# Dividing softmax rows before they are turned, and writing out the order of VectorE and ScalarE, in the second attention of a two-layer network on one core

## The chip, the cores and the metric

One core of one Trainium2 chip, everything in fp32. The metric is the device time of the whole program in microseconds (us): lower is better. The program is one launch that computes a whole network of six parts, from an input of 4096 rows of 256 elements to an output of the same shape.

PE is the engine for matrix products and for transposes (a transpose is a product with the identity). DVE and ACT are the two vector engines: DVE does reductions and arithmetic on tiles, ACT does functions such as the exponential, which can add up its own outputs on the way, and copies. POOL does slower arithmetic and issues the indirect DMAs, SP issues ordinary DMAs. Each engine works through its own instructions in order and waits for the others by semaphores. PE writes into PSUM, of which a bank holds 128 x 512 elements here; the program has two pairs of banks for scores ("s"), three single banks that most other results take in turn ("m") and one for the attention's result ("z").

## The reference, cut to what is computed

```python
x = x + 0.5 * ffn0(ln(x)); x = x + attn0(ln(x)); x = x + 0.5 * ffn0(ln(x))
x = x + 0.5 * moe(ln(x)); x = x + attn1(ln(x)); x = x + 0.5 * moe(ln(x))

def attn1(x, w_q, w_k, w_v, w_o):          # x: 8 x 512 x 256, 16 heads of 64
    q = einsum("bsd,hdk->bhsk", x, w_q)    # k and v alike
    scores = einsum("bhqk,bhmk->bhqm", q, k) / 8
    z = einsum("bhqm,bhmk->bhqk", softmax(scores), v)
    return x + einsum("bse,ed->bsd", join_heads(z), w_o)

def moe(x, ...):                           # 16 experts in 4 groups, 4 chosen of each row
    weights, chosen = top4(softmax(x @ gate_w.T), within the two best groups)
    return sum(weights[e] * ((silu(x @ w1[e]) * (x @ w3[e])) @ w2[e])) + shared(x)
```

`ln` is the layernorm without scale and offset. There is no mask in `attn1`.

## The kernel before

**The six parts.** ffn0, the first attention, ffn0 again, then the first `moe` (the grouped FFN), the second attention and the second `moe`. The rows of the network, 32 tiles of 128 x 256, stay in the core's memory in `self.x`. The parts overlap at their ends. The first `moe` ends with 72 steps of collecting not yet done: for each tile of rows and each of four choices, POOL gathers the rows that an expert has left in DRAM (L1433), and two tiles later DVE adds them, times their weight, to `self.x` (L1452). These steps are handed to the second attention in the list `beside`. The second `moe` in its turn routes its first 20 of 32 tiles inside the second attention: class `Front` normalises rows on POOL (`normal`, `units`), `routing` is a generator of small steps, most of them on DVE, and `send` writes finished rows to the places of their experts by indirect DMAs.

**The second attention** (`_attn1`, L922 to L1162). It is worked in 64 chunks `n`; a chunk is one of eight sequences `b` and one of eight pairs of heads `c`. A chunk has two halves of two query tiles `qt` each. What a chunk needs:

- `heads(n)`: two projections, four matmuls of 128 x 512 each (q and k of two heads, L997), evicted to `qk`.
- `scores(g)` for half-chunk `g`: per query tile two products of 128 x 512 (L1023) into a pair of "s" banks; DVE takes the negated row maxima (L1029), ACT the exponentials of both heads with their row sums (L1032), into tiles `ex`. The exponentials are not divided by their sums.
- `turn(n, qt)`: for each of the two heads four transposes of 128 x 128 (L1044) into an "m" bank, which is evicted to `eT` by `evict`: DVE for head 0 (L189), ACT for head 1 (L187).
- `products(n)`: 16 matmuls (L1057) of the turned exponentials with v into the "z" bank, then the division. `run` takes the reciprocals of the chunk's sums on DVE and widens them on POOL (L1064) so that each stands 64 times; `scale` transposes these to a row per column (four transposes on PE, L1070), copies them out on ACT (L1074) and multiplies the result `zp` by them on DVE (L1076), into `zn`.
- once per sequence: `prepare(b)` normalises four tiles (L957), adds the normalised rows to `self.x` on POOL, turns them (two pieces) and projects v (eight pieces of two matmuls, L978). The moments of the layernorm are taken in lumps, with the first, fourth and sixth sequence (`ln_range`). `project(b)`, four pieces of eight matmuls (L1087), adds the output projection to `self.x`.

**What sets the order.** The loop at the end of `_attn1` is written under `tc.manual_schedule` for PE and POOL: these two run their instructions in the order in which the program writes them. For DVE and ACT a scheduler orders the instructions by its own estimates. In the loop, the scores stand one half ahead of the transposes that use them. In each half PE gets: the scores of the next half, (in a first half) the `products` of the chunk before, the first `turn`, (in a first half) `scale`, one piece of the list `fill`, the second `turn`, then more pieces of `fill`. `fill` holds the projections of the chunk after next, a part of `prepare` of the next sequence in six of eight chunks, the four pieces of `project` of the last sequence, and in five chunks the pieces of `Front.units`. The collecting steps are taken from `beside`, four in each first half from the second chunk on, with a hint that ties each addition to a maximum of the half before (`behind`). Routing takes six steps per chunk at once, after the 48th chunk (`ahead`), and `send` one tile of rows in each of the last 20 halves.

## Time and profile before

| | before |
|---|---|
| median of 3 runs | 4362.0 us |
| lowest, highest | 4359.38, 4363.59 us |
| the profiled execution | 4400.12 us |
| its span (first to last instruction) | 4398.4 us |
| its mean granted clock of PE | 0.915 |
| busy over the span | PE 87%, PE's weight loads 52%, DVE 44%, ACT 33%, POOL 28% |
| the second attention (L922 to L1162) in that span | about 2633 to 3930 us |
| the same stretch, 1297 us long | PE busy 1247.6, DVE 732.3, ACT 583.6, POOL 251.3 us |

The profiled execution is one run with the profiler on, and it lies 38 us above the median of the others. Its rows give, for each group of instructions, how often it ran, the busy time of all of them, the mean time of one in ns, and how long the engine stood idle just before them with what ended that ("the releaser"). A line number is the line of the kernel's source that wrote the instruction; helpers such as `evict` have one line for all their callers, so these groups are told apart by the names of tiles. A timeline's rows give start and length in us. A table of stretches gives the busy time of each engine between two moments of the span, PE's granted clock as a share of full speed, and how busy the DMA was.

### The profile page before, as it was taken

How to read it: one execution, taken by the hardware profiler on the slowest of the kernel's cores; microseconds unless marked ns; L12 is line 12 of the kernel's file. 1: busy time of each engine (PE TensorE's matmuls, PEld its weight loads, DVE VectorE, ACT ScalarE, POOL GpSimd, SP SyncE). 2: the span in 40 equal slices, each digit the busy share in tenths (PEclk: the TensorE clock that was granted, in tenths of full speed). 3: DMA queues.
4: the chain of work that ended last, by engine and by line, in shares of the span. 5: the costliest groups of instructions: out<-in, count | busy, mean ns of one | idle time of the engine just before them, and what ended most of it. 6: DMA issues, size and time to landing. Idle time of an engine off the chain costs nothing.

```text
span 4398.4 us, 51682 instructions
## 1 busy us (share of the span) xinstructions
PE 3847.5 (87%) x17660; PEld 2307.5 (52%) x17660; DVE 1956.4 (44%) x5201; ACT 1440.2 (33%) x3227; POOL 1227.8 (28%) x1132
## 2 busy tenths in 40 slices
PE   5799987999999669999678879999999999998877
PEld 5566563333334546566455754545545555556654
DVE  5221106555544431120564456665555556445354
ACT  2122222444433212222122324444444444443321
POOL 2323223333220123223154241220000111533164
PEclk9999997899985579999789999999999999999998
DMA  5223226500000313222434540110000000135453
GB/s 181 54 58 68 68 35 221 184 22 12 23 20 6 98 34 67 66 61 39 125 128 131 190 148 20 30 29 1 1 1 1 1 1 8 53 116 160 147 173 101
DMA packets 262993, 316.65 MB, mean 72 GB/s; under 512 B 31696, under 2 KB 232784, under 8 KB 262480
## 3 DMA queue, kind: packets, MB, share of 16 engines
q1 hardware_dynamic: 213584, 212.12, 15.5%
q0 software_dynamic: 49152, 101.24, 9.5%
q8 instruction: 146, 2.39, 0.2%
q14 instruction: 111, 0.91, 0.1%
HBM read 157.81 MB, written 147.06 MB: 69 GB/s over the span
## 4 chain that ended last, share of the span: by engine, by line
PE 57%; DVE 9%; issue 8%; ACT 5%; DMA 4%; POOL 2%; another core or an unknown queue 1%; POOLq 0%; DVEq 0%; ACTq 0%; SPq 0%
PE pq L997 5%; PE op L459 5%; PE sp L1023 5%; PE zp L1057 5%; PE hp L448 4%; PE tp L1044 4%; PE hs L1661 3%; PE st L769 3%; PE pv L978 3%; PE hp L1581 2%; PE yp L1087 2%; PE pp L637 2%; ACT ex L1032 2%; DMA acc_d<-ob,idx 2%; PE yps L1681 2%
## 5 line engine op out<-in xcount | busy, mean ns | idle before, releaser
L1032 ACT ACTIVATE ex<-sp,nmax 128x512 f32<-128x512 f32 x512 | 347.8, 689 | 410.9 <-DVE nmax L1029 386.0
L459 PE MATMUL op<-w,hid 128*128 128x256 f32 x2048 | 472.6, 394 | 0.0
L448 PE MATMUL hp<-exT,w 128*128 128x512 f32 x1024 | 448.7, 596 | 0.0
L459 PEld LDWEIGHTS op<-w,hid 128*128 128x128 f32 x2048 | 405.4, 199 | 66.8 <-issue 8.6
L1433 POOL DMA_INDIRECT yg<-ys_d,slot x256 | 264.6, 1034 | 523.4 <-DVE x L1452 246.5
L466 POOL DMA_INDIRECT acc_d<-ob,idx x128 | 199.8, 1561 | 689.0 <-ACT ob L465 391.3
L464 DVE TENSOR_TENSOR ob<-op,b 128x256 f32<-128x256 f32 x128 | 54.3, 424 | 664.0 <-PE op L459 490.2
L1661 PE MATMUL hs<-w_sb,xT 128*128 (+1 forms) x1152 | 321.5, 403 | 24.6 <-ACT xT L1648 9.3
L1029 DVE TENSOR_REDUCE nmax<-sp 128x2 f32<-128x1024 f32 x256 | 303.0, 1218 | 73.8 <-PE sp L1023 72.9
L1044 PEld LDWEIGHTS tp<-ident,ex 128*128 128x128 f32 x2048 | 226.8, 141 | 191.3 <-issue 129.4
L448 PEld LDWEIGHTS hp<-exT,w 128*128 128x128 f32 x1024 | 195.0, 192 | 233.0 <-issue 232.1
L1044 PE MATMUL tp<-ident,ex 128*128 128x128 f32 x2048 | 275.2, 277 | 37.0 <-ACT eT L187 36.5
L740 DVE CUSTOM_DVE_ANT_0 junk<-sp,mask 128x128 f32<-128x128 f32 (+3 forms) x512 | 248.5, 485 | 129.3 <-PE sp L733 109.5
L452 ACT ACTIVATE hid<-hp,b 128x512 f32<-128x512 f32 x256 | 176.0, 687 | 339.2 <-PE hp L448 338.2
L1023 PE MATMUL sp<-qk,qk 64*128 64x512 f32 x1024 | 261.4, 629 | 1.9 <-ACT ex L1032 1.9
L1250 POOL DMA_INDIRECT slots_d<-wide,slot x176 | 173.8, 988 | 298.5 <-DMA slots_d<-wide,slot 110.7
L997 PE MATMUL pq<-xnT,wide 128*128 128x512 f32 x512 | 252.0, 616 | 5.7 <-DVE eT L189 5.0
L778 ACT ACTIVATE ex<-st 128x1024 f32<-128x1024 f32 (+3 forms) x256 | 174.1, 704 | 243.0 <-DVE st L776 243.0
L1661 PEld LDWEIGHTS hs<-w_sb,xT 128*128 128x128 f32 x1152 | 206.0, 199 | 62.9 <-issue 22.4
L1057 PE MATMUL zp<-eT,v 128*64 128x512 f32 x1024 | 234.8, 600 | 0.3 <-DVE eT L189 0.3
L465 ACT ACTIVATE ob<-ob,gate 128x256 f32<-128x256 f32 x128 | 65.0, 508 | 510.0 <-DVE ob L464 482.6
L1064 POOL COPY wide<-rec 128x512 f32<-128x512 f32 x64 | 39.4, 616 | 669.6 <-PE rp L1070 572.3
(326 smaller groups left out, 6105.1 us busy)
## 6 DMA issues: line engine op xcount, KB each, us to landing
xs<-slots_d SPq DMA_DIRECT2D x70, 512.0 KB
ys_d<-ys SPq DMA_DIRECT2D x70, 512.0 KB
w<-in_W SPq DMA_DIRECT2D x32, 1024.0 KB
slots_d<-mask SPq DMA_DIRECT2D x8, 2304.0 KB
ys_d<-mask SPq DMA_DIRECT2D x8, 2304.0 KB
w_sb<-in_w SPq DMA_DIRECT2D x24, 512.0 KB
xn_d<-xn SPq DMA_DIRECT2D x16, 512.0 KB
acc_d<-x SPq DMA_DIRECT2D x8, 1024.0 KB
```

The source lines that it names most:

```text
L448: nc.tensor.matmul(hp, lhsT=w1[:, c, f * P : f * P + P], rhs=exT[e][:, c, h * CH : h * CH + CH], start=(c == 0), stop=(c == DC - 1),)
L459: nc.tensor.matmul(op, lhsT=hid[h][:, f, i * P : i * P + P], rhs=w2[:, f, :], start=(f == 0), stop=(f == FC - 1),)
L466: nc.gpsimd.indirect_dma_start(out=acc_d[:, :], out_offset=bass.IndirectOffsetOnAxis(ap=idx[:, e, st : st + 1], axis=0), in_=ob, in_offset ...
L740: nc.vector.tensor_tensor_reduce(out=junk[:, :wd], in0=sps[h // 2][:, h % 2, :wd], in1=mask[:, S - wd :], scale=1.0, scalar=NEG, op0=ALU.a ...
L997: nc.tensor.matmul(pp, lhsT=(wq, wk)[a][:, k, c * P : c * P + P], rhs=seq[b]["xnT"][:, k, :], start=(k == 0), stop=(k == DC - 1),)
L1023: nc.tensor.matmul(sp[:, j, :], lhsT=q[r, qt * P : qt * P + P], rhs=k[r, :], start=True, stop=True)
L1029: latest[0] = nc.vector.tensor_reduce(nmax, sp, AX.X, ALU.max, negate=True).ins
L1032: nc.scalar.activation(ex[:, j, :], sp[:, j, :], AF.Exp, bias=nmax[:, j : j + 1], accum_out=ch["sums"][:, qt, j : j + 1],)
L1044: nc.tensor.transpose(tp[:, k, :], ch["ex", qt][:, j, k * P : k * P + P], self.ident)
L1057: nc.tensor.matmul(zp[DK1 * j : DK1 * j + DK1, :], lhsT=seq[b]["v", h][:, k, at : at + DK1], rhs=ch["eT"][:, j, k, :], start=(k == 0), sto ...
L1433: inst = nc.gpsimd.indirect_dma_start(out=self.y[t][:, r, :], out_offset=None, in_=self.k.ys_d[:, :], in_offset=bass.IndirectOffsetOnAxis( ...
L1661: nc.tensor.matmul(hp.rearrange("p a i -> p (a i)"), lhsT=st[j]["xT"][:, c, :], rhs=self.w13[:, st[j]["e"], c, :].rearrange("p e i -> p (e ...
```

## The change

All of it is in the second attention and in how `Front` is fed; the mathematics is the same.

- **The division.** A new step `divide(i)` follows the exponentials of each query tile on DVE: a reciprocal of the two sums, and two multiplications of a 128 x 512 row in place, one per head. What the transposes read is then already the softmax. `scale`, the widened reciprocals, their transposes and the product after them are gone; `zp` goes to `zn` by a copy on ACT.
- **The order.** DVE and ACT are now in the manual schedule too, so the program's order holds for all four. To write that order, `scores` takes both maxima and then the exponentials of the first query tile; those of the second (`exps(1)`) stand after the first `turn`, `divide(0)` before the second `turn` and `divide(1)` at the end of the half.
- **The evictions** of turned tiles alternate by query tile and no longer by head: `evict(..., qt)`. The first `turn` of a half is evicted by DVE alone, the second by ACT alone.
- **The filling of PE.** A first half takes one piece of `fill` between its turns as before, and then half of what is over three; the second half takes the rest. `prepare` comes as a list for each chunk: the normalising, then both turned pieces, then one or two v pieces per chunk. `project` comes in two chunks, two pieces in each.
- **Normalising.** The moments of the layernorm are taken two tiles at a time at the ends of given chunks (`own`), and finished at the end of another.
- **Collecting.** The four steps stand in each second half, from the first chunk on, after the next scores and before the first `turn`; the hint is gone.
- **Routing.** One step at each of three places of a half, after `begin + groups`; `units` comes in chunks 43 to 47.

The diff, without empty lines, and cut (`...`) where `normal` only repeats the loop that stood in `norm`; the last change to `Front` removes `stats`, which `own` replaces.

```diff
@@ -943,24 +943,22 @@
         def prepare(b):
             st = seq[b] = {"z": []}
-            def norm(c):
+            def normal():
+                mv, rstd = stats
+                st["xn"] = work.tile([P, QT, D], F32, name="xn", bufs=1)
+                st["xnT"] = work.tile([P, DC, CH], F32, name="xnT")
+                for i in range(QT):
...
+                rows = self.x[:, b * QT : b * QT + QT, :]
+                nc.gpsimd.tensor_tensor(rows, rows, st["xn"], ALU.add)
+            def turned(c):
                 def run():
-                    mv, rstd = stats
-                    if c == 0:
-                        if b in (0, 3, 5):
-                            self.ln_range(pool, stats, b * QT, {0: 3, 3: 2, 5: 3}[b] * QT)
...
-                        rows = self.x[:, b * QT : b * QT + QT, :]
-                        nc.gpsimd.tensor_tensor(rows, rows, st["xn"], ALU.add)
                     tp = psum.tile([P, CH], F32, name="tpn", tag="m", bufs=3)
                     for i in range(QT):
                         nc.tensor.transpose(
@@ -982,9 +980,10 @@
                     nc.vector.tensor_copy(st["v", h][:, i, :], pp)
                 return run
-            return [norm(c) for c in range(DC)] + [
-                value(i, h) for h in range(HK // CH) for i in range(QT)
-            ]
+            v = [value(i, h) for h in range(HK // CH) for i in range(QT)]
+            return [[normal], [turned(0), turned(1)], v[0:2], v[2:3], v[3:4], v[4:6], v[6:7], v[7:8]]
         def heads(n):
             b, c = divmod(n, NC)
@@ -1009,11 +1008,10 @@
         def scores(g):
             n, half = divmod(g, 2)
             ch, q, k = chunk[n], chunk[n][0], chunk[n][1]
-            if half == 0:
-                ch["sums"] = work.tile([P, QT, 2], F32, name="sums", bufs=3)
-            sps = []
+            sps, nmax, sums = [], [], []
             for i in range(2):
                 qt = 2 * half + i
                 sp = psum.tile([P, 2, CH], F32, name="sp", tag="s", bufs=2)
@@ -1024,15 +1022,28 @@
                         sp[:, j, :], lhsT=q[r, qt * P : qt * P + P], rhs=k[r, :], start=True, stop=True
                     )
             for i, sp in enumerate(sps):
-                qt = 2 * half + i
-                nmax = work.tile([P, 2], F32, name="nmax", bufs=4)
-                latest[0] = nc.vector.tensor_reduce(nmax, sp, AX.X, ALU.max, negate=True).ins
-                ex = ch["ex", qt] = work.tile([P, 2, CH], F32, name="ex", bufs=4)
+                m = work.tile([P, 2], F32, name="nmax", bufs=4)
+                nc.vector.tensor_reduce(m, sp, AX.X, ALU.max, negate=True)
+                nmax.append(m)
+                sums.append(work.tile([P, 2], F32, name="sums", bufs=4))
+                ch["ex", 2 * half + i] = work.tile([P, 2, CH], F32, name="ex", bufs=4)
+            def exps(i):
                 for j in range(2):
                     nc.scalar.activation(
-                        ex[:, j, :], sp[:, j, :], AF.Exp,
-                        bias=nmax[:, j : j + 1], accum_out=ch["sums"][:, qt, j : j + 1],
+                        ch["ex", 2 * half + i][:, j, :], sps[i][:, j, :], AF.Exp,
+                        bias=nmax[i][:, j : j + 1], accum_out=sums[i][:, j : j + 1],
                     )
+            def divide(i):
+                rec = work.tile([P, 2], F32, name="rec", bufs=2)
+                nc.vector.reciprocal(rec, sums[i])
+                for j in range(2):
+                    row = ch["ex", 2 * half + i][:, j, :]
+                    nc.vector.tensor_scalar(row, row, rec[:, j : j + 1], None, ALU.mult)
+            exps(0)
+            return exps, divide
         def turn(n, qt):
             ch = chunk[n]
@@ -1042,12 +1053,13 @@
                 tp = psum.tile([P, QT, P], F32, name="tp", tag="m", bufs=3)
                 for k in range(QT):
                     nc.tensor.transpose(tp[:, k, :], ch["ex", qt][:, j, k * P : k * P + P], self.ident)
-                self.evict(ch["eT"][:, j, :, qt * P : qt * P + P], tp, j)
+                self.evict(ch["eT"][:, j, :, qt * P : qt * P + P], tp, qt)
         def products(n):
             b, c = divmod(n, NC)
             ch = chunk[n]
+            box = []
             def run():
                 zp = psum.tile([P, CH], F32, name="zp", tag="z", bufs=1)
@@ -1058,25 +1070,14 @@
                             zp[DK1 * j : DK1 * j + DK1, :], lhsT=seq[b]["v", h][:, k, at : at + DK1],
                             rhs=ch["eT"][:, j, k, :], start=(k == 0), stop=(k == QT - 1),
                         )
-                rec = work.tile([P, QT, 2], F32, name="rec", bufs=3)
-                nc.vector.reciprocal(rec, ch["sums"])
-                wide = work.tile([P, QT, 2, DK1], F32, name="wide", bufs=1)
-                nc.gpsimd.tensor_copy(wide, bc(rec, 3, DK1))
-                ch["wide"], ch["zp"] = wide, zp
-            def scale():
-                rp = psum.tile([P, CH], F32, name="rp", tag="m", bufs=3)
-                for qt in range(QT):
-                    nc.tensor.transpose(
-                        rp[:, qt * P : qt * P + P], ch["wide"][:, qt].rearrange("p h d -> p (h d)"), self.ident
-                    )
-                rs = work.tile([P, CH], F32, name="rs", bufs=1)
-                nc.scalar.copy(rs, rp)
+                box.append(zp)
+            def out():
                 zn = work.tile([P, CH], F32, name="zn", bufs=9)
-                nc.vector.tensor_tensor(zn, ch["zp"], rs, ALU.mult)
+                nc.scalar.copy(zn, box[0])
                 seq[b]["z"].append(zn)
-            return [run, scale]
+            return [run, out]
         def project(b):
             def out(i):
@@ -1094,70 +1095,95 @@
             return [out(i) for i in range(QT)]
         front = Front(self, after, ctx)
-        latest = [None]
         def row_psum(cols):
             t = psum.tile([P, CH], F32, name="row", tag="m", bufs=3)
             return t[:, :cols]
-        steps = after.routing(0, front.lg, front.pool, row_psum, lambda: None)
+        known = []
+        steps = after.routing(0, front.lg, front.pool, row_psum, lambda: known.append(True))
         groups = after.parts[0] // QT
-        def ahead(n):
-            i = n - (NC * groups + 2)
-            if i == 0:
-                front.stats()
-            elif 1 <= i <= groups:
-                return front.units(i - 1, row_psum)
-            elif groups < i:
-                advance(steps, 6)
-            return []
-        with tc.manual_schedule(engines={mybir.EngineType.PE, mybir.EngineType.Pool}):
-            for piece in prepare(0) + heads(0) + heads(1):
+        def moments(pool, stats, t):
+            return lambda: self.ln_moments(pool, stats, t, 2)
+        own = {}
+        for first, tiles, n in ((3 * QT, 2 * QT, 10), (5 * QT, 3 * QT, 25)):
+            for t in range(0, tiles, 2):
+                own[n] = moments(pool, stats, first + t)
+                n += 1
+            own[n] = lambda first=first, tiles=tiles: self.ln_finish(pool, stats, first, tiles)
+        begin = NC * groups + 2
+        for t in range(0, after.parts[0], 2):
+            own[33 + t // 2] = moments(front.pool, after.stats, t)
+        last = own[begin]
+        own[begin] = lambda: (last(), self.ln_finish(front.pool, after.stats, 0, after.parts[0]))
+        E = mybir.EngineType
+        with tc.manual_schedule(engines={E.PE, E.DVE, E.Activation, E.Pool}):
+            self.ln_range(pool, stats, 0, 3 * QT)
+            for piece in sum(prepare(0), []) + heads(0) + heads(1):
                 piece()
-            scores(0)
-            fill, tail, behind = [], [], None
+            exps, divide = scores(0)
+            exps(1)
+            divide(0)
+            divide(1)
+            fill, tail = [], []
             coming = prepare(1)
             for n in range(N):
                 b, c = divmod(n, NC)
                 if c == 0:
-                    coming = prepare(b + 1) if b + 1 < B else []
+                    coming = prepare(b + 1) if b + 1 < B else [[]] * NC
                 if n + 2 < N:
                     fill += heads(n + 2)
-                if c not in (3, 4):
-                    fill += coming[:2]
-                    coming = coming[2:]
-                fill += ahead(n)
+                fill += coming[c]
+                if 1 <= n - begin <= groups:
+                    fill += front.units(n - begin - 1, row_psum)
+                def ahead():
+                    if n > begin + groups:
+                        advance(steps, 1)
                 for half in range(2):
                     g = 2 * n + half
                     if g + 1 < 2 * N:
-                        scores(g + 1)
+                        exps, divide = scores(g + 1)
                     if half == 0 and tail:
                         tail.pop(0)()
-                    if half == 0 and n > 0:
+                    if half == 1:
                         for _ in range(min(TOPK, len(beside))):
-                            beside.pop(0)(behind)
-                    t = 2 * n + half - 2 * N + after.parts[0]
+                            beside.pop(0)()
+                    t = g - 2 * N + after.parts[0]
                     if t >= 0:
+                        assert known
                         front.send(t)
-                    behind = latest[0]
                     turn(n, 2 * half)
+                    more = g + 1 < 2 * N
+                    if more:
+                        exps(1)
                     if half == 0 and tail:
                         tail.pop(0)()
+                    ahead()
                     if fill:
                         fill.pop(0)()
+                    if more:
+                        divide(0)
                     turn(n, 2 * half + 1)
-                    left = 2 - half
-                    for _ in range(-(-len(fill) // left)):
+                    ahead()
+                    for _ in range(len(fill) if half else max(0, len(fill) - 3) // 2):
                         fill.pop(0)()
+                    if more:
+                        divide(1)
+                    ahead()
+                if n in own:
+                    own[n]()
                 tail = products(n)
-                if c == 0 and b > 0:
-                    fill += project(b - 1)
+                if b > 0 and c < 2:
+                    fill += project(b - 1)[2 * c : 2 * c + 2]
             for piece in tail + project(B - 1):
                 piece()
@@ -1815,9 +1841,6 @@
         self.lg = self.pool.tile([P, f.parts[0], E1], F32, name="chosen")
         self.xn = {}
-    def stats(self):
-        self.k.ln_range(self.pool, self.f.stats, 0, self.f.parts[0])
     def normal(self, t, n):
         if t % QT == 0:
```

## The prediction

> **What bounds the kernel now.** First the stages: busy time in stretches of the span. The second attention runs from 2633 to 3930 us; nothing else is edited, so I read only that.
>
> ```profile
> core 0: us, PE busy (x) PEld busy (x) DVE busy (x) ACT busy (x) POOL busy (x), PEclk, DMA share, GB/s
> 2660.00:2821.00 161.00, 154.83 (x724) 77.11 (x722) 107.65 (x173) 83.59 (x205) 41.10 (x43) 0.99 0.09 27
> 3135.00:3291.00 156.00, 152.14 (x714) 80.78 (x712) 82.44 (x114) 71.08 (x178) 7.24 (x9) 1.00 0.00 1
> 3600.00:3797.00 197.00, 186.62 (x868) 98.26 (x868) 124.55 (x203) 88.17 (x221) 47.75 (x50) 0.97 0.06 22
> ```
>
> PE is busy 97% at full clock in the middle line, DVE 53% (67% in the first, where the collecting of the FFN before is mixed in). PE sets this stage: a microsecond counts if it leaves PE's line. So next PE's timeline over one chunk (two heads of one sequence; 64 in all), and its waits from 2660 to 3945:
>
> ```profile
> 3821.61 3.65 PE L1057 MATMUL zp<-eT,v 128*64 128x512 f32 x16
> 3825.20 1.09 PE L1044 MATMUL tp<-ident,ex 128*128 128x128 f32 x8
> 3826.13 0.60 PE L1070 MATMUL rp<-ident,wide 128*128 128x128 f32 x4
> 3826.64 1.99 PE L997 MATMUL pq<-xnT,wide 128*128 128x512 f32 x4
> 3828.46 1.04 PE L1044 MATMUL tp<-ident,ex 128*128 128x128 f32 x8
> 3829.34 1.96 PE L997 MATMUL pq<-xnT,wide 128*128 128x512 f32 x4
> 3831.23 1.99 PE L1023 MATMUL sp<-qk,qk 64*128 64x512 f32 x8
> 3833.14 1.53 PE L1044 MATMUL tp<-ident,ex 128*128 128x128 f32 x12
> 3835.64 0.66 PE L1044 MATMUL tp<-ident,ex 128*128 128x128 f32 x4 [0.97 <-ACT eT L187]
> 3836.22 1.99 PE L1023 MATMUL sp<-qk,qk 64*128 64x512 f32 x8
> ```
>
> ```profile
> PE tp L1044 <- ACT eT L187: 36.5, 37, 2.0
> PE pq L997 <- DVE eT L189: 5.0, 4, 2.6
> ```
>
> From start to start: zp 3.59, eight transposes 0.9, rp 0.51, a projection 1.85, four score matmuls 1.92. There is one hole: the last four transposes find no free bank, because ACT's eviction stands behind exponentials. Sixteen transposes take 3.08 there (3833.14 to 3836.22) where two undisturbed eights take 1.80: 1.28 lost, 37 times. Last the groups of the same stretch that price DVE, and a timeline at 661:
>
> ```profile
> L1029 DVE TENSOR_REDUCE nmax<-sp 128x2 f32<-128x1024 f32 x254 | 300.7, 1218 | 73.4 <-PE sp L1023 72.5 <-issue 0.7
> L1452 DVE SCALAR_TENSOR_TENSOR x<-yg,coef,x 128x256 f32<-128x256 f32 x72 | 34.5, 479 | 1.1
> L957 DVE TENSOR_SCALAR xn<-x,mv,rstd 128x256 f32<-128x256 f32 x24 | 9.2, 406 | 0.0
> ```
>
> ```profile
> 661.45 3.48 DVE L159 TENSOR_SCALAR y<-mv 128x4 f32<-128x4 f32 x1
> 661.64 0.54 POOL L576 MEMSET widek<- 128x512 f32 x1
> ```
>
> **What the Trainium skill says.** VectorE: DVE Perf Modes, section "The perf-mode tier table": fp32 tensor_scalar in SBUF runs two elements per cycle; its errata section measures some 150 cycles fixed, so my estimate for 128x512 is (256+150)/0.96 = 0.42 us. The trace has no such shape; 128x256 with two pointer scalars takes 0.406, which at one element per cycle would leave 0.14 fixed, at two 0.27. I take 0.49, bounds 0.42 and 0.69 (the trace's 128x512 DVE reads from PSUM). SBUF — State Buffer, "Who interferes with whom": such an instruction and a GpSimd one exclude each other. The trace agrees: the 128x4 one above took 3.48 us (median of its line 0.17), until POOL's row of memsets ended at 664.9. TensorEngine Tiling (Array Packing), "Key Properties": a change of tiling mode drains TensorE. The trace shows weight loads 0.76 apart at such changes against 0.24; the change keeps all five of a chunk.
>
> **Removed.** Four rp transposes per chunk, on PE's line: 64 x 0.51 = 32.6. POOL's copy (0.62), ACT's rs copy (0.59, replaced by an equal zn copy) and DVE's zn product and reciprocal (0.69 + 0.20) are not on PE's line: no gain.
>
> **The stalls of 1.28.** Now one projection is placed in each half between the two eights, so sixteen never stand together; the evictions of the first eight are both DVE's, of the second both ACT's, and these stand after both exponentials. Does a new wait replace it? Walk through a half with times from PE's start of scores. DVE reads scores at 1.18 (timeline: 3831.23 to 3832.40), two maxima end at 3.55, evictions of the first eight at 4.2 and 4.85. PE does scores to 1.92, eight transposes to 2.85, projection to 4.7, then needs the bank freed at 4.2, the next at 5.15 (freed 4.85): slack 0.4 and 0.3, no stall. ACT: exponentials 2.4 to 5.2, then its evictions, needed a half later. The scaled rows are needed a half later too. So all of 37 x 1.28 = 47 goes. The few DVE waits (5.0) go as well: sum of gains 85.
>
> **Added on DVE.** A division of a tile: reciprocal 0.17 and two products, 0.49 long but about 0.42 apart: 1.1 us, four per chunk, less 0.9 removed: +3.5 on 82.4/8 = 10.3, so 13.8 against a chunk of about 18.4 (74%). In bulk it lies beside PE. It could delay the maxima: in the first half of a chunk (9.2 long on PE, since zp stands in it) DVE's two divisions end at 7.5 + 2.2 = 9.7, the next half needs it at 10.4. At 0.69 per product 10.9, 0.5 late, 0.1 stall after the slack: at most 6 us over all. Cost taken: 0.
>
> **Moved: the FFN's additions.** 72 of them, four in each second half of chunks 0 to 17, now written between the maxima and the evictions. Before, a scheduler put them in DVE's gaps. Queued behind them: the evictions, and behind those PE's next transposes. The four are chained, 0.5 each (the group's mean is 0.479): first eviction ends at 3.55 + 2.0 + 0.65 = 6.2 instead of 4.2, where PE wants it at 4.7: 1.5, and 0.2 more for the projection's bank. 18 x 1.7 = 31 lost. Bounds: 0.9 each (16) if PE is late there anyway, 2.2 (40) if the gathers' data come late. The gathers themselves, on POOL, only start half a chunk earlier: 0.
>
> **Moved: normalisation and routing.** Moments go to the ends of chunks, two tiles (1.15) each: behind them stand the next maxima, with zp's 3.6 on PE before anything is needed: 0. The three finishing pieces wait for ACT's root behind its evictions; same cover, 2 in all. Normal rows of a sequence start POOL's 2.36 us sum just before a division: 8 times, in a half with slack: 0; POOL's four rows per group of the next FFN (4.84 together) hold divisions up to 2.5: 5 times, I take 1 each, 5. Routing: three steps per half over six chunks, by their rows (0.5 to 1.5 each) some 30 us on DVE, 4.5 to 5 per chunk: DVE then has 18 to 19 against PE's 16.5, and the maxima of the second half begin 2 late. I count 3 in four chunks, 1 in the two whose output projection gives DVE time, 3 for the step with two 128x640 products (2 x 2.3): 17. The lump before cost about 4 beyond the 2.6 counted above; net 13, bounds 4 and 25. The start has one division more before PE's first transposes: 2. The sends of the last ten chunks: POOL needs 7.1 per half (1.22 + 5.76), PE's halves average 7.4; divisions wait up to 1.2 for its rows: 2, and the next FFN's load still has the output projection as cover. SP's queue is unchanged in order.
>
> **Sum.** Gains 85, losses 31 + 2 + 5 + 13 + 2 + 2 = 55: net 30. The profiled execution took 4400.12 (span 4398.4, 1.7 around it), so 4370 in its terms; it lies 38 us over the median of 4362.0, and the 30 us of a stage at full clock I carry over unscaled: 4332.
>
> **Rivals.** (1) The additions cost little, because PE reaches that place late or DVE has caught up: their 31 falls to about 5, routing to 5: 85 - 5 - 5 - 11 = 64, 4298. For it: slack in first halves; against: the order is fixed, maxima cannot begin before 1.18. (2) Order costs more than I see: 0.4 us of slack per half is thin, and if every chunk loses 0.45 to a bank, 64 x 0.45 = 29 brings it to 4361, the same. For it: DVE's maxima and evictions now decide each transposition; against: the walk. (3) Slower: the divisions are the bound. Mechanism: a product of 1.0 us (held by POOL or by waiting for its own reciprocal) makes a division 2.2, the first half's end at 11.9, the maxima 1.5 late, PE 1.1 short in the 48 chunks without output projection: 53 lost, 4385. It decides from about 0.8 per product on: there the loss has taken 30. Against it: L957's 0.406 and no POOL work in chunks 18 to 40. (4) PE was never the limit, and DMA or the gathers end the stage: 97% busy and 1 GB/s speak against it; no number of its own, within the same band.
>
> **Numbers.** Mine 0.55 (4312 to 4350), rival 1 0.20, rival 2 0.13, rival 3 0.10, rival 4 0.02. Range 4290 to 4366: rival 1 with its lower bounds at the bottom, rival 2 at the top. 0.2% (9 us) is about what a measurement can tell from no change: faster than 4353 has 0.55 + 0.20 and a part of rival 2, 0.78; the same 0.11; slower 0.11.
>
> **What would show it.** No rp rows; PE's wait for ACT's eviction near zero; plain chunks of about 14.8 us between zp starts (16.5 now), 147 to 148 per eight against 156; in the first two sequences instead PE waiting for DVE's evictions, about 1.7 per chunk, and eight chunks in 161 to 163; products at 0.42 to 0.5; PE waits on DVE where routing stands. Wrong if the middle sequences do not fall below 150, if products take 0.7 or more, or if a stall per chunk stands in front of the second eight everywhere.

## The result, and the profile after

The changed kernel takes 4328.22 us (median of 6 runs, 4315.64 to 4344.49) against 4359.69 before (6 runs): a ratio of 0.9934, interval [0.9912, 0.9957]. The profiled execution took 4328.61, its span 4326.9. The two profiled spans differ by 71.5 us, but only part of that is the change: 41 us of it lie after the last zp, in the last FFN, which is not edited and where PE was granted 0.91 of its clock before and 0.94 after. (That end takes 488 us before and 447 after, but among the changed kernel's variants below it also ranges from 445 in e1 to 486 in e8.) So from here on the measure is a stretch that holds the edited loop and runs nearly at full clock: from the start of the first zp to the start of the last, chunk by chunk. It is 1233.5 us before and 1205.7 after, 27.8 less; the forecast had 30.

The eight sequences of that stretch, in us (the first has no output projection of an earlier sequence in it; the last has seven steps from zp to zp, the others eight):

| sequence | 1 | 2 | 3 | 4 | 5 | 6 | 7 | 8 | sum |
|---|---|---|---|---|---|---|---|---|---|
| what else is in it | collecting | collecting | collecting's end | | | units | routing | sends | |
| before | 143.7 | 156.6 | 157.4 | 156.0 | 156.0 | 183.8 | 161.8 | 118.4 | 1233.5 |
| after | 148.5 | 163.8 | 149.2 | 147.9 | 147.9 | 176.7 | 159.1 | 112.7 | 1205.7 |

First the busy times in three stretches, the first with collecting, the second without other work, the third with routing:

```profile
core 0: us, PE busy (x) PEld busy (x) DVE busy (x) ACT busy (x) POOL busy (x), PEclk, DMA share, GB/s
2660.00:2821.00 161.00, 147.73 (x668) 70.58 (x668) 127.12 (x234) 78.89 (x198) 36.61 (x35) 0.99 0.09 27
3135.00:3283.00 148.00, 147.36 (x684) 76.92 (x680) 111.00 (x216) 72.41 (x180) 2.37 (x1) 1.00 0.00 1
3608.00:3767.00 159.00, 151.54 (x688) 77.33 (x686) 133.76 (x259) 69.31 (x177) 54.41 (x47) 1.00 0.09 31
```

In the middle line PE is still the bound, at 147.36 of 148 us, and DVE has gone from 53% to 75%. In the first line PE is busy 92% where it was 96% before: something new stops it there, while DVE works 127 of 161 us. PE's timeline over one plain chunk of the changed kernel, from zp to zp, shows the new order; it answers to the timeline of before:

```profile
3268.79 3.65 PE L1069 MATMUL zp<-eT,v 128*64 128x512 f32 x16
3272.38 1.09 PE L1055 MATMUL tp<-ident,ex 128*128 128x128 f32 x8
3273.31 1.88 PE L996 MATMUL pq<-xnT,wide 128*128 128x512 f32 x4
3275.03 1.04 PE L1055 MATMUL tp<-ident,ex 128*128 128x128 f32 x8
3275.99 1.99 PE L1021 MATMUL sp<-qk,qk 64*128 64x512 f32 x8
3277.91 1.09 PE L1055 MATMUL tp<-ident,ex 128*128 128x128 f32 x8
3278.84 1.88 PE L996 MATMUL pq<-xnT,wide 128*128 128x512 f32 x4
3280.56 1.04 PE L1055 MATMUL tp<-ident,ex 128*128 128x128 f32 x8
3281.53 1.99 PE L1021 MATMUL sp<-qk,qk 64*128 64x512 f32 x8
```

No row of rp, no row of 12 and 4 transposes, no idle time in brackets: 14.65 us to the next zp at 3283.44. PE's waits over the whole attention, the first three that concern the loop:

```profile
PE tp L1055 <- DVE eT L189: 32.5, 24, 2.7
...
PE pq L996 <- ACT qk L1002: 4.5, 10, 1.6
PE tp L1055 <- ACT qk L1002: 3.9, 3, 1.3
```

The wait for ACT's evictions (36.5 us, 37 times) is gone, and one for DVE's evictions stands in its place, 32.5 us, 24 times. From 2660 to 2986 alone, the two sequences with collecting, it is 21.2 us, 15 times; in the three sequences after them there is none, and the rest lies in the last three. The two groups of DVE that are new:

```profile
L1043 DVE TENSOR_SCALAR ex<-ex,rec 128x512 f32<-128x512 f32 x508 | 241.9, 518 | 9.0
L1040 DVE RECIPROCAL rec<-sums 128x2 f32<-128x2 f32 x254 | 39.4, 155 | 0.7 <-ACT ex L1033 0.7
```

A multiplication is 0.49 us long (the median; the mean is 0.518), and two of them in a row take 0.88: the second starts 0.40 after the first. With the reciprocal a division is 1.07 us, forecast 1.1. The Trainium skill's page VectorE: DVE Perf Modes, section "The perf-mode tier table", which gives such an operation two elements per cycle in SBUF, is borne out: at one element per cycle 512 elements alone would be 0.53 (512/0.96, an estimate with the clock of that page), more than the whole operation takes.

### The profile page after: what moved, and what is told of

The parts are those of the page before. It is cut to its first block, busy times and chain, and to the rows that moved or that the text cites. A ratio compares the mean times of both kernels' runs of the same rounds, so it can differ in the third digit from the quotient of the medians.

```text
span 4326.9 us, 51707 instructions
## 1 busy us (share of the span) xinstructions
PE 3805.9 (88%) x17404; PEld 2269.2 (52%) x17404; DVE 2148.3 (50%) x5841; ACT 1431.6 (33%) x3227; POOL 1197.4 (28%) x1068
## 4 chain that ended last, share of the span: by engine, by line
PE 30%; DVE 7%; issue 6%; DMA 5%; POOL 3%; ACT 2%; POOLq 0%; DVEq 0%; ACTq 0%; SPq 0%
PE zp L1069 5%; PE sp L1021 4%; PE tp L1055 4%; PE pq L996 4%; DMA yg<-ys_d,slot 3%; PE pv L976 3%; PE yp L1088 2%; POOL slots_d L1276 2%; PE hs L1687 2%; DVE nmax L1026 2%; PE hp L1607 1%; ACT ex L1033 1%; POOL yg L1459 1%; DVE x L1478 1%; PE yps L1707 1%
## 5 line engine op out<-in xcount | busy, mean ns | idle before, releaser
L1055 PE MATMUL tp<-ident,ex 128*128 128x128 f32 x2048 | 280.4, 279 | 37.0 <-DVE eT L189 32.5
L1043 DVE TENSOR_SCALAR ex<-ex,rec 128x512 f32<-128x512 f32 x512 | 243.7, 518 | 9.0
L996 PE MATMUL pq<-xnT,wide 128*128 128x512 f32 x512 | 241.9, 597 | 5.6 <-ACT qk L1002 4.5
```

Of the source, the lines that this page charges most:

```text
L996: nc.tensor.matmul(pp, lhsT=(wq, wk)[a][:, k, c * P : c * P + P], rhs=seq[b]["xnT"][:, k, :], start=(k == 0), stop=(k == DC - 1),)
L1055: nc.tensor.transpose(tp[:, k, :], ch["ex", qt][:, j, k * P : k * P + P], self.ident)
```

## The experiments

Three questions tell the prediction's account from its rivals. Is the removed PE work worth its own time, and nothing else lost for it? Did the order of the turns end the stall, or who evicts? And what costs the time in the first two sequences, the place of the additions or DVE's load? Three groups of runs were made, each with runs of the kernel before beside them; that kernel took 4359.2, 4411.0 and 4404.6 us there, so between groups only ratios and the stretch compare. A ratio is of medians; the sequences are those of one profiled execution of each kernel.

In that execution PE's granted clock drops to one half for 3.4 us or 6.8 us at a time, and its matmuls then take about twice as long (one of zp 1.11 us at most, 0.59 otherwise). Such a stretch costs PE at most half its length. The last column gives the sum of these halves, from the trace's records of the clock: an estimate, and an upper bound, of what each sequence owes to its clock. Sequences 4 and 5 have none in any kernel, and of the third sequences only that with doubled products has one (1.7). Whether a kernel's waits bring the drops about is not shown. All times in us:

| kernel | ratio to before, interval | sequences 1, 2 | 4, 5 | 6 | 7 | 8 | stretch | at most from the clock, sequences 1, 2, 6, 7, 8 |
|---|---|---|---|---|---|---|---|---|
| before | 1 | 143.7, 156.6 | 156.0, 156.0 | 183.8 | 161.8 | 118.4 | 1233.5 | 0, 0, 6.8, 1.7, 0 |
| changed | 0.9934 [0.9912, 0.9957] | 148.5, 163.8 | 147.9, 147.9 | 176.7 | 159.1 | 112.7 | 1205.7 | 0, 1.7, 5.1, 0, 0 |
| e1 additions later | 0.9871 [0.9854, 0.9887] | 135.7, 147.9 | 147.9, 147.9 | 173.4 | 159.1 | 115.3 | 1175.6 | 0, 0, 1.7, 0, 3.4 |
| e2 order alone | 1.001 [1.0, 1.002] | 155.8, 167.7 | 152.1, 152.1 | 172.9 | 158.4 | 111.7 | 1223.1 | 1.7, 1.7, 0, 0, 0 |
| e3 order left to scheduler | 0.9952 [0.9939, 0.9966] | 157.0, 149.0 | 149.0, 149.0 | 178.4 | 160.4 | 110.0 | 1201.9 | 6.8, 0, 10.2, 1.7, 0 |
| e4 evicted by head | 0.9951 [0.9933, 0.9969] | 143.7, 157.4 | 148.9, 148.9 | 185.6 | 162.3 | 114.2 | 1210.2 | 0, 0, 8.5, 1.7, 1.7 |
| e5 turns together | 1.0175 [1.0158, 1.0192] | 167.9, 180.7 | 159.7, 159.8 | 195.6 | 171.0 | 117.8 | 1313.8 | 11.9, 10.2, 11.9, 1.7, 0 |
| e6 products left out | 0.9875 [0.9845, 0.9905] | 151.8, 161.6 | 147.4, 147.4 | 171.7 | 151.4 | 110.3 | 1190.3 | 3.4, 0, 5.1, 0, 0 |
| e6 products doubled | 1.0181 [1.0153, 1.021] | 168.5, 181.3 | 156.0, 155.3 | 196.1 | 174.7 | 125.9 | 1315.2 | 12.1, 13.7, 11.9, 5.1, 5.1 |
| e7 routing covered | 0.9826 [0.98, 0.9852] | 135.5, 147.9 | 147.9, 147.9 | 176.0 | 156.7 | 115.4 | 1175.6 | 0, 0, 4.8, 0.3, 3.4 |
| e8 ten results | 0.9845 [0.9826, 0.9864] | 135.7, 147.9 | 147.9, 147.9 | 173.7 | 159.1 | 109.0 | 1169.5 | 0, 0, 1.7, 0, 0 |
| e9 second head on ACT | 0.9875 [0.9853, 0.9898] | 140.4, 151.7 | 147.4, 147.4 | 175.1 | 163.7 | 108.6 | 1182.7 | 0, 0, 5.1, 3.4, 0 |
| e10 v on ACT | 0.9836 [0.9816, 0.9855] | 135.5, 147.9 | 147.9, 147.9 | 180.6 | 157.9 | 109.0 | 1175.0 | 0, 0, 8.5, 0, 0 |

**e1: the additions behind the evictions.**

```diff
                     if half == 0 and tail:
                         tail.pop(0)()
-                    if half == 1:
-                        for _ in range(min(TOPK, len(beside))):
-                            beside.pop(0)()
...
                     ahead()
                     if fill:
                         fill.pop(0)()
+                    if half == 1:
+                        for _ in range(min(TOPK, len(beside))):
+                            beside.pop(0)()
                     if more:
                         divide(0)
```

> The changed kernel with one thing moved: the four collecting additions of a second half stand behind the evictions of the first eight transposes, ahead of the first division, and not ahead of those evictions. Theory A (what the additions cost is that PE's next transposes wait for DVE evictions queued behind them): the first two sequences fall from 148.4 (seven chunks) and 163.8 us to about 137 and 150, PE's waits for DVE's evictions there (21 us) go, 25 to 28 us in all, about 4302. Rival B (DVE has no room for 2 us more per chunk, wherever they stand; it is busy 115 to 122 of 148 to 164 us there): the wait returns before the maxima or the scaled rows, only 10 to 15 us gained, about 4315. Rival C (the gathered rows come late, so DVE stands at an addition anyway): no change.

Measured: 4300.54 us, and the first two sequences 135.7 and 147.9. The second takes exactly what a sequence without collecting takes, and the first, eight chunks too and 12 us shorter, has no output projection in it, which is 14 us of PE's line elsewhere. Theory A holds, B and C fall. What happens is seen in a second half of the changed kernel, from the end of the maxima, with PE's and DVE's rows in order of time:

```profile
2758.01 1.09 PE L1055 MATMUL tp<-ident,ex 128*128 128x128 f32 x8
2758.95 1.88 PE L996 MATMUL pq<-xnT,wide 128*128 128x512 f32 x4
2759.55 2.04 DVE L1478 SCALAR_TENSOR_TENSOR x<-yg,coef,x 128x256 f32<-128x256 f32 x4
2761.50 1.28 DVE L189 COPY eT<-tp 128x512 f32<-128x512 f32 x2
2762.24 1.25 PE L1055 MATMUL tp<-ident,ex 128*128 128x128 f32 x8 [1.41 <-DVE eT L189]
```

The tile that PE wrote by 2759 is evicted from 2761.5 on, since the four additions (2.04 us) go first; PE finished its projection at 2760.8 and stood idle until 2762.2, when the first bank was free. The same place in e1:

```profile
2739.85 1.09 PE L1055 MATMUL tp<-ident,ex 128*128 128x128 f32 x8
2740.78 1.88 PE L996 MATMUL pq<-xnT,wide 128*128 128x512 f32 x4
2741.38 1.28 DVE L189 COPY eT<-tp 128x512 f32<-128x512 f32 x2
2742.50 1.04 PE L1055 MATMUL tp<-ident,ex 128*128 128x128 f32 x8
...
2743.31 2.04 DVE L1478 SCALAR_TENSOR_TENSOR x<-yg,coef,x 128x256 f32<-128x256 f32 x4
```

The same 2.04 us on the same engine, two evictions later: PE does not stop. DVE's load is the same (121.5 us busy in the second sequence, 121.8 in the changed kernel); only its place differs.

**e2: the order without the row division.** `divide` is emptied, and the division of before stands after zp again:

```diff
-                rec = work.tile([P, 2], F32, name="rec", bufs=2)
-                nc.vector.reciprocal(rec, sums[i])
-                ...
+                pass
...
-                nc.scalar.copy(zn, box[0])
+                rp = psum.tile([P, CH], F32, name="rp", tag="m", bufs=3)
+                ...
+                nc.scalar.copy(rs, rp)
+                nc.vector.tensor_tensor(zn, ch["zp"], rs, ALU.mult)
...
-                if b > 0 and c < 2:
-                    fill += project(b - 1)[2 * c : 2 * c + 2]
+                if b > 0 and c == 0:
+                    fill += project(b - 1)
```

> The changed kernel's order of all four engines, with the division of before: rows stay undivided, reciprocals are widened on POOL, transposed on PE, copied on ACT and multiplied in on DVE; the output projection's four pieces stand in one chunk as before. Theory A (the two halves of the change add up, and the divisions cost PE nothing): PE gets 64 x 0.51 = 32.6 us back, eight plain chunks take 152 in place of 148, about 4361. Rival B (the divisions load DVE so that PE is late elsewhere, in the additions and the routing): part of the 32.6 is given back, about 4345. Rival C (without the row division the order itself loses, the new product waiting on ACT holds DVE): over 4370.

Measured: 4362.94 us (18 runs), no better than before; plain sequences take 152.1, 4.2 more than the changed kernel, which is about eight times 0.51. So in plain sequences A holds. But sequences 6 to 8 are 3.8, 0.7 and 1.0 us faster than in the changed kernel, although the 4 us stand in them too. Something that the divisions bring costs PE 8, 5 and 5 us there; in the sixth up to 5 of the 8 are PE's clock, in the eighth a part can be another wait (e8 below). That is rival B's point, in the last three sequences alone. The stretch says 17.4 us between the two kernels, the ratios 33 with an uncertainty of about 11; the profiled execution of e2, at 4349.13 us, is the fastest of its 18 and 14 us under their median, so its stretch may be shorter than usual; where those 14 us lie is not shown.

**e4 and e5: who evicts, and where the projection stands.** The edit of e4 is `self.evict(..., tp, j)` in place of `qt`. In e5 the first piece of `fill` moves behind the second turn (and zn has eleven buffers, which is left out here):

```diff
-                    if fill:
-                        fill.pop(0)()
                     if more:
                         divide(0)
                     turn(n, 2 * half + 1)
                     ahead()
+                    if fill:
+                        fill.pop(0)()
```

> The changed kernel, with the turned tiles evicted by head again (one on DVE, one on ACT in each turn). Theory A (the stall went because one projection now stands between the two eights; which engine evicts matters little): PE's waits at the transposes stay near zero in the middle sequences, eight plain chunks 148 to 149, within 10 us of the changed kernel. Rival B (the stall went because the first turn's evictions are on DVE alone): PE waits for ACT's evictions again, about 1 us in each second half, 64 us, about 4390.

> The changed kernel with the piece of filling work behind the second turn, so that sixteen transposes stand together in every half, evicted by query tile as in the changed kernel; two more buffers for the normalised results, since the order needs them. Theory A (three banks for four tiles: the last four transposes wait for the first eviction, which cannot come before both maxima): about 1.0 to 1.2 us lost in each second half, where zp does not cover it, 64 to 77 us, about 4395, eight plain chunks 156 to 157. Rival B (evicting the first turn on DVE alone, ahead of the exponentials' queue, is enough): at most 10 us.

With eviction by head nothing returns: 148.9 and no wait for ACT's evictions of turned tiles in sequences 3 to 5. It even loses less to the additions (143.7 and 157.4 us in the first two sequences), probably because one of the two evictions behind them has gone to ACT; its median of 4340.71 is within the uncertainty of the changed kernel's. With the turns together the stall is back, and larger than either theory had it: 159.7 per plain sequence, 1.48 per chunk. PE's timeline of a plain second half of e5 shows all of it:

```profile
3355.53 1.53 PE L1055 MATMUL tp<-ident,ex 128*128 128x128 f32 x12
3357.80 0.66 PE L1055 MATMUL tp<-ident,ex 128*128 128x128 f32 x4 [0.74 <-DVE eT L189]
3358.40 1.98 PE L996 MATMUL pq<-xnT,wide 128*128 128x512 f32 x4
3360.31 1.99 PE L1021 MATMUL sp<-qk,qk 64*128 64x512 f32 x8
```

Sixteen transposes take 2.87 (3355.53 to 3358.40) where the changed kernel's two eights take 0.93 + 0.97: 0.97 lost. Each projection takes 1.91 ahead of scores, and 1.72 between two turns: 0.19, twice a chunk. The rest, 0.14, is in the first half. So the place of the projection is what ended the stall; which engine evicts hardly matters.

**e6: what the divisions cost.** Once with the two multiplications left out, so that the softmax stays undivided in that kernel, and once with each followed by a multiplication by 1.0:

```diff
                     row = ch["ex", 2 * half + i][:, j, :]
                     nc.vector.tensor_scalar(row, row, rec[:, j : j + 1], None, ALU.mult)
+                    nc.vector.tensor_scalar(row, row, 1.0, None, ALU.mult)
```

> The changed kernel with the two multiplications of each division left out and the reciprocals kept, so the softmax stays undivided and only its time is read. It asks what the divisions cost PE. Theory A (nothing where DVE has room, something where other work shares DVE): eight plain chunks stay at 148; the first two sequences and the three with units, routing and sends fall, by some 17 us in all over the last three (what the runs with and without row division differ there beyond PE's transposes). Rival B (they cost nothing anywhere): within 5 us of the changed kernel. Rival C (they cost a bank's wait in each half): plain chunks fall too, under 146 per eight.

> The changed kernel with each multiplication of a division followed by a second one by 1.0, so a division is 1.93 us and not 1.05. It asks where the divisions become the bound. Theory A (the walk of the prediction: divisions end late in the first half of a chunk and push the next maxima): about 0.7 us per chunk lost, eight plain chunks 153, some 40 us over all, more in the sequences with additions and routing. Rival B (DVE has 37 us per eight chunks to spare and takes the 28 more in it): plain chunks stay under 150. Rival C (DVE's sum becomes the bound): over 160.

Left out, plain sequences go from 147.9 to 147.4, and sequences 6, 7 and 8 fall by 5.0, 7.7 and 2.4, 15.1 together where 17 was expected. That is theory A, but not in the first two sequences, which were to fall too: the first rises by 3.3, as much as its clock costs, and the second falls by 2.2, of which up to 1.7 is clock. Doubled, plain sequences take 155.3 to 156.0, 0.97 more per chunk (0.7 expected), and the whole stretch is 109 us longer, not 40. Of these up to 43 are PE's clock; with the clock taken off, each sequence loses 5 to 13, the plain ones 7 to 8. DVE is busy 137 of 156 us in a plain one, so its sum isn't the bound there; its order is. In a second half of that kernel:

```profile
3344.12 1.99 PE L1021 MATMUL sp<-qk,qk 64*128 64x512 f32 x8
...
3346.95 2.35 DVE L1026 TENSOR_REDUCE nmax<-sp 128x2 f32<-128x1024 f32 x2
...
3349.95 1.25 PE L1056 MATMUL tp<-ident,ex 128*128 128x128 f32 x8 [1.10 <-DVE eT L189]
```

The maxima could start 1.18 us after the scores do, as the prediction read from the kernel before, so at 3345.3. They start at 3346.95, when the divisions are done, and PE waits 1.10 for the evictions behind them. This is rival 3's mechanism, as written; it shows with a division of about 1.9 us, and the real one is 1.07.

**e3: DVE and ACT given back to the scheduler.**

```diff
-        with tc.manual_schedule(engines={E.PE, E.DVE, E.Activation, E.Pool}):
+        with tc.manual_schedule(engines={E.PE, E.Pool}):
```

> The changed kernel with DVE and ACT out of the hand-written order of the second attention: a scheduler orders their instructions, as before; PE and POOL keep theirs. Theory A (the fixed order of DVE brings nothing by itself and loses where the additions stand in it): additions fall into gaps, the first two sequences take about 137 and 150 us, the middle ones 148, about 4302. Rival B (without the fixed order evictions and divisions stand in each other's way): PE waits at the transposes again, plain chunks over 152, 4350 or more.

Neither. Plain sequences lose 1.1 us, the second one is free of the additions' cost as A said, but the first takes 157.0, by two chunks of 26.9 and 28.7: there the scheduler puts additions whose gathered rows have not come ahead of evictions, and PE waits 5.0, 3.7 and 3.9 us for those. At about the end of each of these three waits the clock drops to half, which costs up to 6.8 us more. In sum it is 3.8 us shorter than the changed kernel over the stretch, although its clock takes up to 12 us more there, and it is not to be told from it by the ratio. So the written order of DVE and ACT is worth 1.1 us in a plain sequence, and the changed kernel lost that again by where it puts the additions.

**e7: routing's steps moved** (on top of e1), from the ends of first halves, where nothing covers the next maxima, to the second turn and to the ends of second halves.

```diff
                     if half == 0 and tail:
                         tail.pop(0)()
-                    ahead()
...
                     turn(n, 2 * half + 1)
                     ahead()
+                    ahead()
...
-                    ahead()
+                    if half == 1:
+                        ahead()
+                        ahead()
```

> The kernel with the additions behind the evictions, and with the routing's steps moved: none at the end of a first half, ahead of maxima that no zp covers, and none between the first turn and the first piece; two behind the second turn of each half and two at the end of the second half. Theory A (the steps ahead of uncovered maxima and evictions are what routing costs PE): the seventh sequence falls from 159 to about 152, 5 to 8 us, about 4294. Rival B (DVE's sum is the bound there, 16 to 18.6 of 20 us busy): no change, 159.

Sequence 7 falls by 2.4 us, half of the least that theory A asked for, and sequence 6, whose last chunk already holds the first steps, rises by 2.6: the stretch is 1175.6 in both. But that rise is no more than what PE's clock takes there (4.8 for 1.7 us), so a gain of some 2.4 us by the moved steps is possible and not shown. Neither theory is borne out: most of routing's cost stays when its steps move between these places.

**e8, e9, e10: the results' buffers, and DVE relieved** (all on top of e1). e8 has `bufs=10` for zn. e9 and e10 have that too; in e9 the second head's multiplication is `nc.scalar.activation(row, row, AF.Copy, scale=rec[:, j : j + 1])`, in e10 v is evicted by `nc.scalar.copy`.

> The kernel with the additions behind the evictions, and ten buffers in place of nine for the normalised results zn. In the changed kernel ACT's copy of the second result of each sequence waits up to 5 us for the output projection to free a buffer (43 us in all), and evictions on ACT stand behind it. Theory A (that wait is covered, the budget of PE shows no hole there): the stretch between the first and the last zp stays at 1175 to 1176 us, eight plain chunks 148. Rival B (it delays PE in each sequence): 0.5 to 1 us per sequence, 4 to 8 us in all.

> The kernel with the additions behind the evictions and ten results, and with one of the two multiplications of each division, that of the second head, moved from DVE to ACT (a copy with a scale per row, some 0.6 us). DVE is relieved of 14 us per eight chunks, ACT gets 19 more on 72. Theory A (what is still lost in the sequences with units, routing and sends is DVE's sum): routing's sequence falls from 159 to 155, that of the units from 174 to 171, the last a little, plain ones stay at 148; stretch about 1166. Rival B (on ACT the rows come behind its queue of exponentials and evictions, too late for the next turn): plain chunks rise over 150, stretch 1190 or more.

> The kernel with the additions behind the evictions and ten results, and with the evictions of v moved from DVE to ACT (eight per sequence, 0.69 us each on DVE, some 0.6 on ACT). It gives DVE 5.5 us per eight chunks without touching the divisions. Theory A (DVE's sum sets what is lost in the loaded sequences): routing's sequence falls from 159 by 2 to 4 us, plain ones stay at 148. Rival B (v's bank comes free later behind the exponentials): PE waits for a bank at each v, 0.3 us or more, plain sequences 150 or more.

e8: neither. Seven sequences don't move; the eighth goes from 115.3 to 109.0, of which up to 3.4 is PE's clock in e1. ACT's waits in the changed kernel, over the attention, show where it came from:

```profile
ACT zn L1077 <- PE yp L1088: 42.9, 7, 11.8
```

ACT's copy to zn needs a buffer that the output projection frees, and in six sequences that wait (about 5 us) is covered. In the last, no v projections fill PE and the wait is 11.8 us; ACT's evictions stand behind it. In e1 it is 12.8, and in e8 the row is gone. Between e8 and the changed kernel, neither with a drop of the clock there, sequence 8 differs by 3.7. e9 misses: ACT takes the rows without harm to plain chunks (147.4), but routing's sequence takes 163.7, with one chunk of 25.7 for 19.1, and sequences 1 and 2 lose 4.7 and 3.8 us, where PE now waits for v's evictions on DVE (3.5 us) and for those of turned tiles on ACT (2.5). In the long chunk PE waits for a bank:

```profile
3675.89 3.78 PE L976 MATMUL pv<-wide,xnT 128*128 128x512 f32 x4 [4.74 <-DVE qk L1004]
```

DVE's eviction of this bank stands behind routing's two products of 128 x 640 and their sums, 4.6 us together, and from about the end of the wait PE's clock is at half for 6.9 us. In e8 the same step stands ahead of the same eviction, but there v's product takes a bank that ACT has emptied and waits 0.31; what makes it take the other bank in e9 is not shown. Relieving DVE of 14 us per eight chunks did not buy what leaving the products out did, so for routing DVE's sum is not the whole cause. What the rest of routing's cost is stays open. e10 gains 1.2 in sequence 7, where 2 to 4 were expected, and its loss of 6.9 in sequence 6 is no more than its clock there. By their ratios e7, e8 and e10 (0.9826, 0.9845 and 0.9836) are the lowest and can't be told from each other; the shortest stretch is that of e8.

## Why the prediction was right, and where its terms were off

The time was forecast at 4332 and came out at 4328; the medians differ by 31.5 us and the stretch by 27.8, for a forecast of 30. The mechanism is shown: PE's line sets the stage, rp and the stall leave it, and the additions give part back. But both columns of the sum were too large, and that their errors cancelled is luck. By e1 and e8 and the plain sequences, the losses below are 40, not 55, and the gains 27.8 plus these, 67, not 85. PE's clock, which takes up to 8.5 us of the stretch before and 6.8 after, makes the terms of sequences 6 and 7 uncertain by 2 us each.

- **PE bounds the stage, DVE has room: right.** DVE 75% in a plain sequence, forecast 74%; plain chunk 14.65 us, forecast 14.8; eight chunks 147.9, forecast 147 to 148.
- **rp, 32.6: right.** 4.08 us of PE's line per plain sequence before, none after; e2 puts 4.2 back.
- **The stalls, 47 and 5: the mis-sized term.** Added up kind by kind, PE's line in sequence 4 lost 4.1 by rp and 4.0 by all else, so 32 over eight sequences, not 52. A stall was worth 1.18 and not 1.28: two eights now take 0.93 + 0.97, not 1.80, and 0.97 is what an eight takes whenever scores follow it. Four stalls stand in a plain sequence (4.7 us). And there is a new wait, not foreseen: twice a sequence PE waits for ACT's eviction of qk or its bank, some 0.5 each. The projections, shorter where transposes follow them (1.72 for 1.82) as e5 shows, give 0.85 back. The trace had the better number: 36.5 us of idle time, 37 times.
- **The additions, 31: right in place and size.** e1 takes them away at 12.8, 15.9 and 0.8 in the first three sequences, 29.5, of which up to 1.7 is clock.
- **Routing, net 13: too large.** Sequence 7 gained 2.7 where a plain one gains 8.1: 5.4 net. The lump before cost 5.8 (161.8 for 156.0), or 4.1 without its one drop of the clock, which is the 4 taken; the spread steps cost 11.2, not 17. So the net is between 5.4 and 7.1. e6 shows that 7.7 of them come only together with the divisions.
- **Units 5, sends 2: too large.** Sequence 6 gained 7.1, so the units cost about 1, or 2.7 with the clock taken off on both sides; sequence 8, with e8's buffers, gains 9.4, so the sends cost nothing. The start and the finishing of the normalisation, 2 each, were not measured apart.
- **Missed: the zn buffer.** The new copy on ACT waits for a free buffer; 3.7 us in the last sequence. The forecast costed that copy as equal to the rs copy it replaces, and did not ask what its output waits for.
- **Rival 1** (4298) had the right size of what the additions could give, for another kernel: e1, at 4300.5, is that case made on purpose. **Rival 2** fell: it needs 0.45 in every chunk, and a plain sequence has two waits of some 0.5 in its eight chunks. **Rival 3** is a real mechanism (e6 doubled), shown with a division near twice as long. Its limits in the prediction are off by its own numbers: at 0.69 per product the divisions end at 7.5 + 2 x 1.55 = 10.6, not 10.9, and with the 0.4 of slack taken off the loss reaches 30 at 0.9 per product, not 0.8. Rival 4 fell with e1 and e2, which follow PE's line.
- **A reading that was too wide:** in the prediction's own trace the weight loads stand 0.76 or 0.81 apart at four of the five changes of tile shape in a chunk; from transposes to scores it is 0.17. Nothing in the sum rests on it.

## What to carry to other kernels

When an order is written out by hand, ask of every instruction what is queued behind it on its engine and who waits for that: 2.04 us of DVE work cost up to 2 us a chunk ahead of two evictions, and nothing behind them. Take the value of a stall from the idle time that the trace shows, and rebuild the line after the change kind by kind, since the neighbours of each instruction change too. A right total doesn't prove its terms; the sequences with and without each piece of other work do.

## What was not expected of the hardware

POOL's sum of a sequence's rows held a multiplication on DVE for nearly its whole length. The changed kernel's DVE and POOL at the start of a sequence:

```profile
3283.81 2.35 POOL L958 TENSOR_TENSOR x<-x,xn 128x1024 f32<-128x1024 f32 x1 [145.51 <-DVE rec L1040]
3283.84 3.00 DVE L1043 TENSOR_SCALAR ex<-ex,rec 128x512 f32<-128x512 f32 x2
```

Two multiplications take 3.00 us where they take 0.88 elsewhere, 2.12 more, nearly POOL's 2.35. The Trainium skill's page SBUF — State Buffer, section "Who interferes with whom", says this of such a multiplication and a POOL instruction: the one that issues first holds the ports they share for its whole length, and the other waits. Here POOL starts at 3283.81 and DVE at 3283.84. It happens in five sequences, and in the one shown zp covers it: PE's next transposes start at 3287.03, when zp is done. And a projection of four matmuls took 1.72 us of PE's line in a plain sequence of the changed kernel when transposes (tiles of 128 x 128) followed it and 1.91 when scores (tiles of 64 x 128) did; in the kernel before, most took 1.82 ahead of transposes and 1.89 ahead of scores. Eight transposes took 0.87 to 0.93 ahead of a projection of q or k, 0.97 ahead of scores.
